# Cross attention in seven-product form: the values with channels on the partitions, turned by VectorE and ScalarE

## The chip, the cores and the metric

The kernel runs on one core of a Trainium2 chip. A core has a matrix engine (TensorE, PE in the profile, with its weight loads shown as PEld), a vector engine (VectorE, DVE), an activation engine (ScalarE, ACT), a general engine (GpSimd, POOL) and a queue engine (SyncE, SP), each with its own instruction stream; DMA queues move data between them. Engines wait for each other through semaphores. The metric is the device time of one execution in microseconds, of which the median over several runs is taken.

## The reference

There are 32 batch items, each with C = 256 channels and N = 1024 positions, all in float32. Cut to what matters:

```python
x_q = einsum('oc,bcn->bno', w_qk, y)          # y is ctx_2048
x_k = einsum('oc,bcn->bon', w_qk, x)
x_v = einsum('oc,bcn->bon', w_v, x) + b_v[None, :, None]
energy = einsum('bnc,bcm->bnm', x_q, x_k)
attention = softmax(energy, axis=-1)
attention = attention / (1e-07 + attention.sum(axis=1, keepdims=True))
x_r = einsum('bcn,bnm->bcm', x_v, attention)
x_r = relu(einsum('oc,bcn->bon', w_t, x - x_r) + b_t[None, :, None])
return x + x_r
```

## The kernel before

The weights are folded once at the start: `w_qk` with itself for the keys, and `w_t` with `w_v` for the values, so that the values already carry the last projection. Each batch item then has four products: keys (`Keys`, tiles `pg` and `gx`), values (`Values`, tiles `pu` and `ut`), energies (`Energy`, tiles `pe` and `e`, in four steps t = 0 to 3 of 128 rows per half) and the attention with the projected input (`Attention`, tiles `po`, `et`, `z`). Every one of them is cut into two by two blocks and computed with seven block products instead of eight. That is why every class has the steps p1 to p7 for products and c11, c12, c21, c22 for the blocks of the result: some products are accumulated onto others in the same PSUM bank, and between two of them ScalarE copies the bank to SBUF (`p1s`, `p5s`, `w`). A product that is accumulated onto a bank therefore waits until ScalarE has copied that bank.

The factors of the seven products are sums of blocks. For the input they are `xs` and `ys`, made by DMAs: SP loads copies, and GpSimd's queue then issues three DMAs that add (`accumulate`; the steps `xsteps` and `ysteps`). For the keys they are `gt`, for the values `us`, four additions on GpSimd each. For the attention they are `et`, additions on VectorE (`mix`).

The attention multiplies the values as weights (128 positions on the partitions, 128 channels as columns) with rows of `e` as moving data. It therefore wants the values with positions on the partitions. The kernel before makes them so at once: `Values.product` takes a 128 by 128 slice of the input as weights and the folded weights (128 columns) as moving data, four times for one block product. The bias of the values, a row of 256 numbers, is spread over the partitions (`uc`) and added to the whole tile `ut` by one accumulating DMA from GpSimd's queue (`bias`).

The order of the work is written out by hand: the wrappers `pe`, `dve`, `act` and `pool` (`InOrder`) keep each engine's instructions in the order in which the main loop calls them. All of them are recorded on line 77, so the profile's groups are told apart by tiles. The main loop over the batch items `b` first runs the energies of item b in the four steps t; at t = 0 the rest of the attention of the item before is mixed in (`before.end()`, `before.c21()`), and so is the next load of `x`. The keys of item b+1 follow, and its values, and then the attention of item b (`begin` and `run`), inside which the last value product (`u.p4`) and value blocks of item b+1 are made. For the last item, b = 31, there is nothing to prefetch: `more` is false, `before.end()` is not called at t = 0, and its attention and the rest of item 30's follow at the end.

In one item VectorE makes the energies' blocks (which also yield row minima and maxima), the weighted column sum `acc`, the column scale `rc`, the scaling of `e` (`normal`), the sums `et` and the output blocks `z`, which SP stores.

Of the kernel before, what the change touches and what calls it, by code (L numbers as in the profile page):

```python
# [9 lines left out]
F32 = mybir.dt.float32  # L10
# [6 lines left out]
def kernel(  # L17
# [29 lines left out]
    nc = tc.nc  # L47
    B, C, N = x.shape
    P = 128
# [16 lines left out]
    class InOrder:  # L66


        def __init__(self, engine):
            self.engine = engine  # L70
            self.last = None
# [37 lines left out]
    def accumulate(into, from_):  # L109
        return pool.dma_start(into, from_, accum_op=ALU.add)  # L110
# [13 lines left out]
    bv = scratch[:, 4, :KC].rearrange("p (k o) -> p k o", o=1)  # L124
    bt = const.tile([P, KC, 1], F32, name="bt")
    nbt = const.tile([P, KC, 1], F32, name="nbt")
    uc = const.tile([P, 1, C], F32, name="uc")
    nc.sync.dma_start(wqk, w_qk.rearrange("(k p) c -> p k c", p=P))
    load("x", 0, KC)
    nc.sync.dma_start(wt, w_t.rearrange("(k p) c -> p k c", p=P))  # L130
# [7 lines left out]
    few = const.tile([P, P], F32, name="few")  # L138
    dve.memset(few, 0.0)
    dve.memset(zeros, 0.0)  # L140
    parts = const.tile([P, NB, NG + 1], F32, name="parts")
    dve.memset(parts[:, :, NG], EPS)
    idle = bank("idle")
# [41 lines left out]
    def value_weights(wtT):  # L185

        pw = [bank(f"pw_{i}") for i in range(KC)]
        for i in range(KC):
            for k in range(KC):
                pe.matmul(  # L190
                    pw[i][:, :C], wv[:, k, ts(i, P)], wtT[:, k, :], start=(k == 0), stop=(k == KC - 1)
                )
        return lefts("wvtT", pw, -1.0)[1]

    bvb = scratch[:, 6, : KC * P].rearrange("p (k c) -> p k c", k=KC)

    def spread_bias():
        for k in range(KC):
            act.activation(bvb[:, k, :], few, AF.Identity, bias=bv[:, k, :], scale=1.0)

    def value_bias(wtT):

        pb = bank("pb")
        for k in range(KC):
            pe.matmul(
                pb[:, :C], bvb[:, k, :], wtT[:, k, :], start=(k == 0), stop=(k == KC - 1)
            )
        act.mul(uc[:, 0, :], pb[:, :C], -1.0)
        act.mul(nbt[:, :, 0], bt[:, :, 0], -1.0)

    up = ctx.enter_context(tc.tile_pool(name="up", bufs=2))
# [4 lines left out]
    def temp(tag, name):  # L216
        return cp.tile([P, MB], F32, tag=tag, name=name)

    def matmul(into, lhs, rhs, onto=False):
        pe.matmul(into, lhs, rhs, start=not onto, stop=True, skip_group_check=onto)  # L220
# [114 lines left out]
    class Values(Seven):  # L335


        def __init__(self, b, xr):
            super().__init__("u", b)
            self.xr = xr  # L340
            self.ut = up.tile([P, NT, C], F32, tag="ut", name=f"ut_{b}")

        def product(self, into, j, onto=False):
            for t in range(HT):
                pe.matmul(
                    into[:, ts(t, P)],
                    self.xr[j - 1][:, ts(t, P)],
                    u_left[j - 1],
                    start=(t == 0 and not onto),
                    stop=(t == HT - 1),  # L350
                    skip_group_check=True,
                )

        def tiles(self, p):
            return p.rearrange("p (t c) -> p t c", t=HT)

        def block(self, i, h):
            return self.ut[:, h * HT : h * HT + HT, ts(i, P)]

        def combine(self, i, h, in0, in1, op):  # L360
            dve.tensor_tensor(self.block(i, h), self.tiles(in0), self.tiles(in1), op)

        def c21(self):
            act.copy(self.block(1, 0), self.tiles(self.one))

        def bias(self):
            accumulate(self.ut, uc.to_broadcast([P, NT, C]))

        def factors(self):

            us = up.tile([P, 4, HT, P], F32, tag="us", name=f"us_{self.b}")
            s1, s2, s3, s4 = (us[:, j] for j in range(4))
            a11, a12, a21, a22 = (self.block(i, h) for i in range(2) for h in range(2))
            steps = [
                lambda: pool.tensor_tensor(s1, a21, a22, ALU.add),
                lambda: pool.tensor_tensor(s2, s1, a11, ALU.subtract),
                lambda: pool.tensor_tensor(s3, a11, a21, ALU.subtract),
                lambda: pool.tensor_tensor(s4, a12, s2, ALU.subtract),
            ]
            return (a11, a12, s4, a22, s1, s2, s3), steps  # L380

    class Energy(Seven):

# [55 lines left out]
    class Attention(Seven):  # L439
# [76 lines left out]
        def run(self, u, before=None):  # L516


            self.normal(0, 0)
            self.normal(1, 0)  # L520
            for j in range(HT // 2):
                self.normal(0, 1, j)
                self.mix(self.t1, self.b11, self.b12, ALU.add, j)
            if u:
                u.c22()
            if before:
                before.put()
                before.c21()
            self.normal(1, 1)
            self.mix(self.t2, self.t1, self.b22, ALU.subtract)  # L530
            self.epart(self.one, 1)
            self.p1s = self.biased(self.one, "p1s", bt[:, 0, :])
            self.epart(self.three, 2)
            self.epart(self.two, 5)
            self.p5s = self.biased(self.two, "p5s", bt[:, 1, :])
            self.xpart(self.one, 6, True)
            if u:
                u.p4()
                u.c21()
                u.c11()  # L540
                u.c12()
            self.c11()
            self.put()
            self.xpart(self.two, 3, True)
            self.epart(self.two, 3, (0, 1))
            self.epart(self.one, 6)
            self.w = self.biased(self.one, "w", nbt[:, 0, :])
            self.mix(self.t3, self.b12, self.b22, ALU.subtract)
            self.mix(self.t4, self.b21, self.t2, ALU.subtract)
            self.epart(self.two, 3, (2,))  # L550
            if u:
                self.epart(self.two, 3, (3,))
                self.c12()

        def end(self):
            self.xpart(self.one, 4, True)
# [57 lines left out]
    g.c11()  # L614
    g.p6()
    wtT, t_left = turned_weights()
    spread_bias()
    g.p3()
    g.c12()
    g.p7()  # L620
    g.c22()
    u_left = value_weights(wtT)
    g.p4()
    g.c21()
    rhs, _ = summed("y", 0)
# [6 lines left out]
    u = Values(0, xr)  # L632
    u.p1()
    u.p5()
    value_bias(wtT)
    u.p2()
    u.c11()
    u.p6()
# [6 lines left out]
    for b in range(B):  # L645
# [3 lines left out]
        for t in range(HT):  # L649
            now = Energy(b, t, lhs, rhs)  # L650
            pair.append(now)
            now.p1()
            if t > 0:
                pair[t - 1].exp(1)
            now.p5()
            if t == 0:
                if b == 0:
                    u.p4()
                    u.c21()
                    u.bias()  # L660
                    xsteps[1]()
                    xsteps[2]()
                elif more:
                    before.end()
                    before.c21()
                    load("x", b + 1)
                e = ep.tile([P, NT, N], F32, tag="e", name=f"e_{b}")
                acc = one.tile([P, N], F32, tag="acc", name=f"acc_{b}")
                ur, usteps = u.factors()
                first = 1 if more else 0  # L670
                for step in usteps[:first] + gsteps + usteps[first:]:
                    step()
            if t > 1:
                pair[t - 2].share(0)
            if t == 0:
                now.p6()
            now.p2()
            now.c11()
            if t == 1:
                pair[0].scale(1)  # L680
            if t > 1:
                pair[t - 1].share(1)
            if t > 0:
                now.p6()
            if t == 1:
                act.activation(acc, e[:, HT, :], AF.Copy, scale=scales[HT])
            if t > 0:
                pair[t - 1].p4()
                pair[t - 1].c21()
                pair[t - 1].exp(0)  # L690
            now.p3()
            now.c12()
            now.p7()
            now.c22()
            if more and b > 0:
                if t == 0:
                    xn, xsteps = summed("x", b + 1)
                else:
                    xsteps[t - 1]()
        last = pair[-1]  # L700

        if more:
# [46 lines left out]
        if more:  # L749
            now = Attention(b, xr, ur)  # L750
            now.begin()
            ysteps[0]()
            now.run(un)
            if b + 2 < B:
                now.xpart(now.one, 7, True)
                now.epart(now.one, 7)
                now.c22()
                now.put()
            now.put()
            ysteps[1]()  # L760
            un.bias()
            ysteps[2]()
            before = now
            xr, u = xn, un
        else:
            before.end()
            now.run(None, before)
            now.finish()
# [30 lines left out]
```

## Time and profile before

| | before |
|---|---|
| median of 3 runs | 2141.78 us (2140.91 to 2142.71) |
| the profiled execution: its time | 2142.63 us |
| the profiled execution: its span | 2140.9 us |
| PE busy | 2134.6 us (100%) |
| VectorE busy | 1769.1 us (83%) |
| ScalarE busy | 788.5 us (37%) |
| GpSimd busy | 612.7 us (29%) |
| granted TensorE clock | 1.000 |
| DMA moved | 282.58 MB |

The span runs from the first to the last instruction; 1.7 us of the profiled execution's time lie around it. "Idle before" in a row is the time for which the engine had nothing to do just before the instructions of the group, followed by what ended it. Times in a timeline are us from the span's start. A float32 product of 512 columns shows as two MATMUL rows, and a VectorE or ScalarE row can overlap the next one by some 0.1 us, since instructions are pipelined.

### The profile page before, as it was taken

The page shows a single profiled execution, that of the slowest core. Times are in us where ns is not written, and L with a number is a line of the kernel's source. Part 1 is how long each engine was busy: PE and PEld are TensorE (multiplying, and loading weights), DVE is VectorE, ACT ScalarE, POOL GpSimd, SP SyncE. Part 2 cuts the span into 40 slices and gives each one's busy share as a digit, 9 for nine tenths or more (in the row PEclk, how much of TensorE's full clock was granted, in tenths as well). Part 3 has the DMA queues.
Part 4 walks back from the last instruction along what each step waited for, and adds up shares of the span by engine and source line. Part 5 has one row for each costly group of instructions (what it writes and reads, how often), then busy time and mean ns, then how long its engine had stood idle before and what let it go on. Part 6 is the DMA issues. An engine that isn't in the chain of part 4 may idle for free.

```text
span 2140.9 us, 19900 instructions
## 1 busy us (share of the span) xinstructions
PE 2134.6 (100%) x6312; PEld 1058.5 (49%) x6312; DVE 1769.1 (83%) x3119; ACT 788.5 (37%) x1323; POOL 612.7 (29%) x488
## 2 busy tenths in 40 slices
PE   9999999999999999999999999999999999999999
PEld 5455444554445545455544555445554445544453
DVE  5889788898788887879878788778897888978898
ACT  5234443244432344333443234442244422444332
POOL 5322323313233133232232322323223233222320
PEclk9999999999999999999999999999999999999999
DMA  6555665556665556665566655665546655566540
GB/s 176 120 127 119 154 151 123 129 120 150 148 126 135 117 144 148 128 151 106 137 151 138 139 113 128 157 144 126 125 121 153 157 121 125 121 154 148 123 98 30
DMA packets 139048, 282.58 MB, mean 132 GB/s; under 512 B 9152, under 2 KB 42688, under 8 KB 138944
## 3 DMA queue, kind: packets, MB, share of 16 engines
q0 software_dynamic: 75936, 114.83, 34.0%
q1 hardware_dynamic: 63008, 166.48, 23.5%
q8 instruction: 50, 0.82, 0.2%
q14 instruction: 54, 0.44, 0.1%
HBM read 181.67 MB, written 33.55 MB: 101 GB/s over the span
## 4 chain that ended last, share of the span: by engine, by line
PE 98%; DVE 2%; issue 0%; DVEq 0%
PE po L77 44%; PE pe L77 35%; PE pu L77 9%; PE pg L77 9%; DVE e L77 1%; DVE acc L77 0%; PE idle L77 0%; DVE et L77 0%; PE pw L77 0%; DVE z L77 0%; DVE rc L77 0%; DVE sc L77 0%; PE pb L77 0%; DVE ri L77 0%; DVE parts L77 0%
## 5 line engine op out<-in xcount | busy, mean ns | idle before, releaser
L77 PE MATMUL pe<-gt,ys 128*128 128x512 f32 x768 | 392.1, 592 | 0.0
L77 DVE SCALAR_TENSOR_TENSOR e<-e,ri,rc 128x512 f32<-128x512 f32 x512 | 347.3, 745 | 1.1
L77 PE MATMUL po<-et,us 128*128 128x512 f32 x768 | 345.7, 593 | 0.5 <-DVE et L77 0.5
L77 DVE SCALAR_TENSOR_TENSOR acc<-e,ri,acc 128x1024 f32<-128x1024 f32 x224 | 288.6, 1288 | 8.0
L77 PE MATMUL pe<-gx,y 128*128 128x512 f32 x512 | 261.4, 592 | 0.0
L77 PEld LDWEIGHTS po<-et,us 128*128 128x128 f32 x768 | 145.5, 190 | 185.0 <-issue 166.8
L77 PEld LDWEIGHTS pe<-gt,ys 128*128 128x128 f32 x768 | 145.8, 190 | 183.4 <-issue 170.0
L77 PE MATMUL po<-e,ut 128*128 128x512 f32 x512 | 224.9, 592 | 0.0
L77 POOL TENSOR_TENSOR gt<-gx 128x512 f32<-128x512 f32 x64 | 81.6, 1274 | 391.4 <-DVE gx L77 391.4
L77 ACT COPY ep1s<-pe 128x512 f32<-128x512 f32 x128 | 75.0, 586 | 303.4 <-PE pe L77 298.9
L77 ACT ACTIVATE e<-e,nm 128x1024 f32<-128x1024 f32 x128 | 147.1, 1149 | 98.2 <-DVE nm L77 96.7
L77 DVE TENSOR_TENSOR et<-e 128x1024 f32<-128x1024 f32 x128 | 156.8, 1246 | 2.3
L77 PEld LDWEIGHTS po<-e,ut 128*128 128x128 f32 x512 | 97.3, 190 | 122.5 <-issue 106.2
L77 PEld LDWEIGHTS pe<-gx,y 128*128 128x128 f32 x512 | 97.2, 190 | 122.0 <-issue 114.1
L77 POOL TENSOR_TENSOR us<-ut 128x512 f32<-128x512 f32 x64 | 87.0, 1360 | 223.9 <-DMA ut<-uc 223.9
L77 ACT ACTIVATE e<-e,bias 128x1024 f32<-128x1024 f32 x128 | 147.4, 1152 | 1.6 <-DVE bias L77 1.5
L77 POOL DMA_DIRECT2D ut<-uc x32 | 50.5, 1579 | 338.0 <-DVE ut L77 281.1
L77 DVE TENSOR_TENSOR z<-z,x 128x512 f32<-128x512 f32 x31 | 46.3, 1492 | 118.3 <-ACT z L77 118.3
L77 DVE CUSTOM_DVE_ANT_0 e<-pe,ep1s 128x512 f32<-128x512 f32 x128 | 88.1, 688 | 64.2 <-ACT e L77 57.8
L77 PE MATMUL pe<-gx,ys 128*128 128x512 f32 x256 | 130.9, 593 | 0.5 <-DVE nm L77 0.5
L77 PE MATMUL pe<-gt,y 128*128 128x512 f32 x256 | 130.8, 592 | 0.0
L77 PE MATMUL po<-e,us 128*128 128x512 f32 x256 | 120.5, 592 | 0.0
(115 smaller groups left out, 3265.5 us busy)
## 6 DMA issues: line engine op xcount, KB each, us to landing
y<-in_ctx_dram SPq DMA_DIRECT2D x32, 1024.0 KB, 5.0
ut<-uc POOLq DMA_DIRECT2D x32, 1024.0 KB, 9.6
out_dram<-z SPq DMA_DIRECT2D x128, 256.0 KB, 2.3
x<-in_x_dram SPq DMA_DIRECT2D x31, 1024.0 KB, 6.2
xs<-in_x_dram SPq DMA_DIRECT2D x62, 512.0 KB, 4.6
ys<-in_ctx_dram SPq DMA_DIRECT2D x62, 512.0 KB, 4.2
xs<-in_x_dram POOLq DMA_DIRECT2D x31, 512.0 KB, 8.1
xs<-xs POOLq DMA_DIRECT2D x31, 512.0 KB, 5.0
```

Of the source, the lines that this page charges most:

```text
L77: self.last = getattr(self.engine, name)(*args, **kwargs)
```

## The change

The values are made with channels on the partitions, as the keys are: `Values.product` uses the folded weights as stationary data and 512 columns of the input as moving data, one product instead of four. The bias is then one number per partition, so ScalarE adds it while it copies the banks (`bu`, `nbu`, made at the start by `value_bias`), and `uc`, its spreading and the accumulating DMA are gone.

The attention still wants positions on the partitions. `turn` therefore has VectorE transpose the four value blocks in squares of 32 by 32 into the tile `turned`: four instructions of 128x512, behind the output block c12 in `Attention.run`. `move` then puts each group of 32 partitions where it belongs: 16 copies of 32x16x32 back into `ut`. For b = 0 SP issues them as 16 DMAs. For every other item ScalarE makes them in the energies of that item at t = 0: 6 ahead of p1's copy, 4 behind p5's copy, 6 behind c22.

GpSimd's order changes with it: a copy of one column (`behind`) makes its additions `gt` wait for VectorE's `t4`; then come the first accumulating DMA for `xs` and the four additions `us`, at the end of t = 0 in place of its beginning. The other two accumulating DMAs for `xs` are issued at t = 2 and t = 3 (before, the three were issued at t = 1, 2 and 3).

```diff
--- before.py
+++ after.py
@@ -124,7 +124,8 @@
     bv = scratch[:, 4, :KC].rearrange("p (k o) -> p k o", o=1)
     bt = const.tile([P, KC, 1], F32, name="bt")
     nbt = const.tile([P, KC, 1], F32, name="nbt")
-    uc = const.tile([P, 1, C], F32, name="uc")
+    bu = const.tile([P, KC, 1], F32, name="bu")
+    nbu = const.tile([P, KC, 1], F32, name="nbu")
     nc.sync.dma_start(wqk, w_qk.rearrange("(k p) c -> p k c", p=P))
     load("x", 0, KC)
     nc.sync.dma_start(wt, w_t.rearrange("(k p) c -> p k c", p=P))
@@ -138,6 +139,7 @@
     few = const.tile([P, P], F32, name="few")
     dve.memset(few, 0.0)
     dve.memset(zeros, 0.0)
+    behind = const.tile([P, 1], F32, name="behind")
     parts = const.tile([P, NB, NG + 1], F32, name="parts")
     dve.memset(parts[:, :, NG], EPS)
     idle = bank("idle")
@@ -192,20 +194,20 @@
                 )
         return lefts("wvtT", pw, -1.0)[1]
 
-    bvb = scratch[:, 6, : KC * P].rearrange("p (k c) -> p k c", k=KC)
-
-    def spread_bias():
-        for k in range(KC):
-            act.activation(bvb[:, k, :], few, AF.Identity, bias=bv[:, k, :], scale=1.0)
-
     def value_bias(wtT):
 
         pb = bank("pb")
-        for k in range(KC):
-            pe.matmul(
-                pb[:, :C], bvb[:, k, :], wtT[:, k, :], start=(k == 0), stop=(k == KC - 1)
-            )
-        act.mul(uc[:, 0, :], pb[:, :C], -1.0)
+        for i in range(KC):
+            for k in range(KC):
+                pe.matmul(
+                    pb[:, i : i + 1],
+                    wtT[:, k, ts(i, P)],
+                    bv[:, k, :],
+                    start=(k == 0),
+                    stop=(k == KC - 1),
+                )
+        act.mul(nbu[:, :, 0], pb[:, :KC], 1.0)
+        act.mul(bu[:, :, 0], pb[:, :KC], -1.0)
         act.mul(nbt[:, :, 0], bt[:, :, 0], -1.0)
 
     up = ctx.enter_context(tc.tile_pool(name="up", bufs=2))
@@ -335,40 +337,52 @@
     class Values(Seven):
 
 
+
         def __init__(self, b, xr):
             super().__init__("u", b)
             self.xr = xr
-            self.ut = up.tile([P, NT, C], F32, tag="ut", name=f"ut_{b}")
+            self.ut = up.tile([P, KC, MH, MB], F32, tag="ut", name=f"ut_{b}")
 
         def product(self, into, j, onto=False):
-            for t in range(HT):
-                pe.matmul(
-                    into[:, ts(t, P)],
-                    self.xr[j - 1][:, ts(t, P)],
-                    u_left[j - 1],
-                    start=(t == 0 and not onto),
-                    stop=(t == HT - 1),
-                    skip_group_check=True,
-                )
-
-        def tiles(self, p):
-            return p.rearrange("p (t c) -> p t c", t=HT)
+            matmul(into, u_left[j - 1], self.xr[j - 1], onto)
+
+        def bias(self, tag):
+            return {"p1s": bu[:, 0, :], "w": nbu[:, 0, :], "p5s": bu[:, 1, :]}[tag]
+
+        def kept(self, p, tag):
+            s = temp(tag, f"u{tag}_{self.b}")
+            act.activation(s, p, AF.Identity, bias=self.bias(tag), scale=1.0)
+            return s
 
         def block(self, i, h):
-            return self.ut[:, h * HT : h * HT + HT, ts(i, P)]
+            return self.ut[:, i, h]
 
         def combine(self, i, h, in0, in1, op):
-            dve.tensor_tensor(self.block(i, h), self.tiles(in0), self.tiles(in1), op)
+            dve.tensor_tensor(self.block(i, h), in0, in1, op)
 
         def c21(self):
-            act.copy(self.block(1, 0), self.tiles(self.one))
-
-        def bias(self):
-            accumulate(self.ut, uc.to_broadcast([P, NT, C]))
+            act.activation(self.block(1, 0), self.one, AF.Identity, bias=bu[:, 1, :], scale=1.0)
+
+        def turn(self):
+
+            self.turned = one.tile([P, KC * MH, MB], F32, tag="turned", name=f"turned_{self.b}")
+            for i in range(KC):
+                for h in range(MH):
+                    dve.transpose(self.turned[:, i * MH + h], self.block(i, h))
+            self.moves = [(a, g) for a in range(NG) for g in range(NG)]
+
+        def move(self, count, by):
+
+            from_ = self.turned.rearrange("p b (k c) -> p (b k) c", c=G32)
+            to = self.ut.rearrange("p i h (k c) -> p (i h k) c", c=G32)
+            from_, to = (v.rearrange("p (k g) c -> p k g c", g=NG) for v in (from_, to))
+            for a, g in self.moves[:count]:
+                by(to[ts(g, G32), :, a, :], from_[ts(a, G32), :, g, :])
+            self.moves = self.moves[count:]
 
         def factors(self):
 
-            us = up.tile([P, 4, HT, P], F32, tag="us", name=f"us_{self.b}")
+            us = up.tile([P, 4, MB], F32, tag="us", name=f"us_{self.b}")
             s1, s2, s3, s4 = (us[:, j] for j in range(4))
             a11, a12, a21, a22 = (self.block(i, h) for i in range(2) for h in range(2))
             steps = [
@@ -377,7 +391,10 @@
                 lambda: pool.tensor_tensor(s3, a11, a21, ALU.subtract),
                 lambda: pool.tensor_tensor(s4, a12, s2, ALU.subtract),
             ]
-            return (a11, a12, s4, a22, s1, s2, s3), steps
+            return [
+                f.rearrange("p (t c) -> p t c", t=HT)
+                for f in (a11, a12, s4, a22, s1, s2, s3)
+            ], steps
 
     class Energy(Seven):
 
@@ -551,6 +568,7 @@
             if u:
                 self.epart(self.two, 3, (3,))
                 self.c12()
+                u.turn()
 
         def end(self):
             self.xpart(self.one, 4, True)
@@ -614,12 +632,12 @@
     g.c11()
     g.p6()
     wtT, t_left = turned_weights()
-    spread_bias()
     g.p3()
     g.c12()
     g.p7()
     g.c22()
     u_left = value_weights(wtT)
+    value_bias(wtT)
     g.p4()
     g.c21()
     rhs, _ = summed("y", 0)
@@ -632,7 +650,6 @@
     u = Values(0, xr)
     u.p1()
     u.p5()
-    value_bias(wtT)
     u.p2()
     u.c11()
     u.p6()
@@ -649,6 +666,8 @@
         for t in range(HT):
             now = Energy(b, t, lhs, rhs)
             pair.append(now)
+            if t == 0 and b > 0:
+                u.move(6, act.copy)
             now.p1()
             if t > 0:
                 pair[t - 1].exp(1)
@@ -657,18 +676,22 @@
                 if b == 0:
                     u.p4()
                     u.c21()
-                    u.bias()
+                    u.turn()
+                    u.move(16, nc.sync.dma_start)
                     xsteps[1]()
                     xsteps[2]()
-                elif more:
+                else:
+                    u.move(4, act.copy)
+                if b > 0 and more:
                     before.end()
                     before.c21()
                     load("x", b + 1)
                 e = ep.tile([P, NT, N], F32, tag="e", name=f"e_{b}")
                 acc = one.tile([P, N], F32, tag="acc", name=f"acc_{b}")
-                ur, usteps = u.factors()
-                first = 1 if more else 0
-                for step in usteps[:first] + gsteps + usteps[first:]:
+                if before is not None:
+
+                    pool.tensor_copy(behind, before.t4[:, HT - 1, :1])
+                for step in gsteps:
                     step()
             if t > 1:
                 pair[t - 2].share(0)
@@ -692,11 +715,16 @@
             now.c12()
             now.p7()
             now.c22()
-            if more and b > 0:
-                if t == 0:
+            if t == 0:
+                u.move(6, act.copy)
+                ur, usteps = u.factors()
+                if more and b > 0:
                     xn, xsteps = summed("x", b + 1)
-                else:
-                    xsteps[t - 1]()
+                    xsteps[0]()
+                for step in usteps:
+                    step()
+            elif more and b > 0 and t > 1:
+                xsteps[t - 1]()
         last = pair[-1]
 
         if more:
@@ -758,7 +786,6 @@
                 now.put()
             now.put()
             ysteps[1]()
-            un.bias()
             ysteps[2]()
             before = now
             xr, u = xn, un
```

## The prediction

> **What bounds the kernel now.** I read the page's engine totals first, then the chain that ended last, then one item on the timeline, engine by engine, and last the two odd items at the ends. The totals and the chain's shares say that TensorE is never idle:
>
> ```profile
> PE 2134.6 (100%) x6312; PEld 1058.5 (49%) x6312; DVE 1769.1 (83%) x3119; ACT 788.5 (37%) x1323; POOL 612.7 (29%) x488
> ...
> PE 98%; DVE 2%; issue 0%; DVEq 0%
> ```
>
> The chain in order of time gives the price of one product. Four key products (8 records) take 3.43, 0.858 each; five value products (40 records) take 4.46, 0.892 each:
>
> ```profile
> 1110.96 3.43 PE pg L77 x8
> 1114.40 4.46 PE pu L77 x40
> ```
>
> So an item takes 70 x 0.858 + 7 x 0.892 = 66.3 us, and 1060.38 to 1126.72 (ScalarE's `op1s` of two items) is 66.34: no stall is left. Anything removed from PE is gained only if no other engine is late instead.
>
> VectorE comes next. From 1111.00, where it waits for p4 of t = 3, it runs without a gap until the second half of `et`; the weights that need it are loaded late, yet the next product is on time:
>
> ```profile
> 1111.00 0.75 DVE L77 CUSTOM_DVE_ANT_0 e<-pe,zeros,nm 128x512 f32<-128x512 f32 x1
> ...
> 1130.05 1.22 DVE L77 TENSOR_TENSOR et<-e 128x1024 f32<-128x1024 f32 x1
> ```
>
> ```profile
> 1131.33 0.19 PEld L77 LDWEIGHTS po<-et,us 128*128 128x128 f32 x1 [0.38 <-DVE et L77]
> ```
>
> A load normally shows 0.24 of idle, so this one is 0.14 late. In the first item the same load is 0.42 late (0.66 against 0.24), and its six products take 2.84 instead of 2.74: 0.10 lost, so 0.32 of lateness is free, and 0.18 of that is unused in an ordinary item.
>
> **The values' products.** Seven per item, 0.034 saved on each: 0.24 per item, 7.7 over 32. Six of the seven lie between 1111.00 and 1131.33, so PE comes 0.21 earlier to a VectorE that does not. 0.18 is free; 0.03 becomes a stall. Left per ordinary item: 0.21. Items 1 to 30 give 6.3. Item 0 uses up its free lateness already and gives only the seventh product, but the seven ahead of the loop give 0.24: together 0.3. In the prologue `pb` (17.59 to 18.46, 0.87) becomes four products of one column; between nothing and 0.87 saved, I take 0.4, since a record does not vanish with its columns. Gain 7.0.
>
> **The bias.** Four ScalarE copies per item turn from 0.586 to 0.687 (`op1s`' row, which has a bias too). `up1s` ends 0.1 later at 1116.07; p6 on that bank starts at 1116.91. The others have the same 0.8. Nothing. The accumulating DMA and GpSimd's wait for it go, and nothing on the path waited for them.
>
> **The transposes** go behind c12 on VectorE, where it idles:
>
> ```profile
> 1077.44 0.68 DVE L77 TENSOR_TENSOR z<-po,ow 128x512 f32<-128x512 f32 x1
> 1080.96 0.69 DVE L77 TENSOR_TENSOR z<-op5s,po 128x512 f32<-128x512 f32 x1 [2.84 <-PE po L77]
> ```
>
> The nearest row transposes 1024 columns, and at full price while GpSimd adds:
>
> ```profile
> 1119.44 1.25 DVE L77 STREAM_TRANSPOSE rc<-sc 128x1024 f32<-128x1024 f32 x1
> ```
>
> ```profile
> 1119.04 1.26 POOL L77 TENSOR_TENSOR gt<-gt,gx 128x512 f32<-128x512 f32 x1
> ```
>
> Half of it is 0.60 to 0.72, start to start 0.64: 1078.04 + 4 x 0.64 + 0.08 = 1080.7, inside the hole. Queued behind them are c22 and the two `put`s, with idle time until 1087.69 after them. Cost on VectorE's path: 0; without that hole it would be 2.6 per item.
>
> The Trainium skill speaks against this choice: "VectorE: DVE Perf Modes", sections "The three transpose paths" and "Rules for kernel authors", sends a full 128x128 transpose to TensorE, because VectorE turns only 32x32 blocks. The trace has it: the prologue's four transposes `pt` took 0.44 of PE (11.07 to 11.51), 0.11 each. By the rule 16 per item would put 1.8 on the engine that is never idle, 56 us in all; by the rows the way chosen costs the path nothing.
>
> **The moves.** ScalarE around the items' border:
>
> ```profile
> 1081.86 0.59 ACT L77 COPY ep1s<-pe 128x512 f32<-128x512 f32 x1 [6.16 <-PE pe L77]
> 1082.73 0.58 ACT L77 COPY ep5s<-pe 128x512 f32<-128x512 f32 x1 [0.28 <-PE pe L77]
> 1086.97 0.69 ACT L77 ACTIVATE z<-po,bt 128x512 f32<-128x512 f32 x1 [3.65 <-PE po L77]
> 1087.83 0.59 ACT L77 COPY ew<-pe 128x512 f32<-128x512 f32 x1 [0.17 <-PE pe L77]
> 1091.32 0.58 ACT L77 COPY ep1s<-pe 128x512 f32<-128x512 f32 x1 [2.90 <-PE pe L77]
> 1091.80 1.15 ACT L77 ACTIVATE e<-e,bias 128x1024 f32<-128x1024 f32 x1
> ```
>
> No row has a ScalarE copy from SBUF across partitions. The nearest is a copy of 512 from PSUM: 0.586, the next starting 0.48 later (1091.32, 1091.80). Reading SBUF adds 0.02 (`xb` 0.711 against 0.687). So 0.48 to 0.61 apart; I take 0.50, as all rows here overlap. All moves need all four transposes: start 1080.75. Six moves, the copies of p1 and p5, four moves: 1080.75 + 10 x 0.50 + 2 x 0.48 = 1086.7, and `z` is due at 1086.8 (PE 0.2 earlier). p1's copy is late, but p6, which waits for it, comes only at 1086.77, behind item b-1's last five products. After `ew` (1087.65) six moves: 1087.65 + 0.48 + 3.0 = 1091.13, p1's copy of t = 1 due at 1091.1. p6 of t = 1 starts at 1092.6, so that copy may start as late as 1091.87. With moves m apart it starts at 1082.77 + 16m: a stall from m = 0.57. At 0.50: 0.
>
> **GpSimd.** The new copy `behind` waits for VectorE's `t4` (1077.52); `gt`, the first `xs` DMA and `us` are queued behind it. `gt` still moves from 1083.35 to 1077.7, earlier than its users (p3 and p7 at 1088.5 and 1089.3), and off the `put`s that it lengthens now (2.36 for two, against 1.37). The first `xs` DMA needs SP's loads (landing at 1089.5, SP's issues being no later than now), then `us` runs from 1091.2 to 1096.3; VectorE's next operation with two SBUF inputs, `acc`, is at 1097.56, so they miss each other by 1.2. 0.
>
> **Item 0.** Two transposes wait for the block of 24.89; VectorE's next, 26.73, slips by 0.1 ahead of a wait of 1.65. SP issues 16 DMAs (0.35 each by its rows, 6 us) from 27; `us` was at 38.5, its first use is at 68.4. 0.
>
> **Item 31** has no cover. There `before.end()` is not called, so p6 of t = 0 comes straight after p5, at 2073.24, half way through the four records of the PE row, while VectorE is still at `et`:
>
> ```profile
> 2067.95 5.47 DVE L77 TENSOR_TENSOR et<-e 128x1024 f32<-128x1024 f32 x2
> 2073.34 2.35 DVE L77 TENSOR_TENSOR et<-e,et 128x1024 f32<-128x1024 f32 x2
> ```
>
> ```profile
> 2072.38 2.03 PE L77 MATMUL pe<-gt,ys 128*128 128x512 f32 x4
> ```
>
> Without GpSimd's collision (5.47 for 2.35; `behind` removes it) `et` ends at 2072.5, the transposes at 2075.7, six moves at 2078.8, p1's copy at 2079.35, p6 at 2079.5: 6.3 of stall, behind which everything is queued. Four moves ahead of `ew` add 0.4 at p7. Stalls of 0.25 there today are swallowed. Loss 6.4.
>
> **Sum.** 2142.63 - 7.0 + 6.4 = 2142.0 for the profiled execution, whose time is 0.85 above the median of the runs: 2141.2. A measurement of this kernel can tell about 0.2%, 4.3 us, from no change.
>
> **Rivals.** *ScalarE overruns (slower).* Place: the last six moves of t = 0 ahead of p1's copy of t = 1, from m = 0.57. At 0.586 the copy is 0.28 late, 8.4 us over 30 items, 2149.6; at 0.61 0.66 late, 20 us, 2161. For it: no row has this form. Against: consecutive ScalarE rows all overlap by 0.1. The same 1.1 us of spare time (16 x 0.07) is eaten if the transposes are 0.9 apart. Chance 0.20.
> *The last item does not stall (faster).* If ScalarE reached p1's copy in time the sum would be 2134.8. For it: the same moves are hidden in 30 items. Against: VectorE's `et` alone reaches 2072.5. Chance 0.08.
> *Item 0's DMAs are late.* They go in runs of 128 bytes; each us past about 63, where `us` must begin, is lost once: up to 10 us, 2151. For: no row shows such a DMA above 72 bytes and below 1 KB. Against: 30 us of cover. Chance 0.10, half of it inside 4.3 us.
>
> **Numbers.** The forecast has 0.62. Its own range, from 0.1 per item either way, is 2138 to 2145: 0.50 unchanged, 0.05 faster, 0.07 slower. With the rivals: faster 0.05 + 0.08 = 0.13, same 0.50 + 0.05 = 0.55, slower 0.07 + 0.20 + 0.05 = 0.32. The range of 8 in 10 runs from 2136, which leaves out the second rival, to 2151, which takes in the third and the near end of the first.
>
> **What would show it.** Right: `pu` products at 0.858, transposes near 0.7 behind c12, moves 0.50 apart, items of 66.1, and a ScalarE row `ep1s` with PE waiting some 6 us near 2070. Wrong: items above 66.4 with PE waiting for ScalarE at t = 1, VectorE rows of `acc` longer than 1.29, GpSimd's first `us` after 63, or no wait in item 31.

## The result, and the profile after

The changed kernel takes 2180.6 us (median of 6 runs, 2179.43 to 2181.54), beside 2141.98 us of the kernel before (6 runs measured together with them). The ratio is 1.018 with a 95% interval of 1.0167 to 1.0193: slower by 38.6 us, where 2141.2 us, no change, was predicted. The profiled execution has a span of 2177.7 us at a granted clock of 0.998.

The totals and the shares of the chain, from the page of the changed kernel:

```profile
PE 2145.1 (99%) x4972; PEld 933.7 (43%) x4972; DVE 1793.1 (82%) x3247; ACT 1096.0 (50%) x1818; POOL 540.0 (25%) x487
PE 69%; ACT 17%; DVE 11%; issue 2%; ACTq 0%; DVEq 0%
```

TensorE still looks busy for 99% of the span, and its busy time has even grown with 1340 instructions fewer, since rows behind a wait are drawn longer (1.13 for 1.02 in the row of p6 below). What tells is the chain. Before, 98% of it was TensorE. Now ScalarE has 17% and VectorE 11%, and among the lines on the page `ACT ut` alone has 14%: the moves decide when the kernel ends. Their group, and the products that wait for ScalarE (columns: busy time and mean ns of one, then the idle time before them and what ended most of it):

```profile
L77 PE MATMUL pe<-gt,ys 128*128 128x512 f32 x768 | 398.7, 601 | 26.4 <-ACT ep1s L77 18.8
L77 ACT COPY ut<-turned 32x512 f32<-32x512 f32 x496 | 305.3, 615 | 164.5 <-DVE turned L77 158.3
```

One move lasts 0.615 on the average, and 496 of them take 305.3. That is 0.615 each also when busy time is divided by their number, so they do not overlap at all. ScalarE around the border of two items, from its timeline; these rows answer to the six shown in "The moves":

```profile
1093.84 3.76 ACT L77 COPY ut<-turned 32x512 f32<-32x512 f32 x6 [5.12 <-DVE turned L77]
1097.62 0.59 ACT L77 COPY ep1s<-pe 128x512 f32<-128x512 f32 x1
1098.10 0.59 ACT L77 COPY ep5s<-pe 128x512 f32<-128x512 f32 x1
1098.72 2.50 ACT L77 COPY ut<-turned 32x512 f32<-32x512 f32 x4
1101.24 0.69 ACT L77 ACTIVATE z<-po,bt 128x512 f32<-128x512 f32 x1
1101.82 0.58 ACT L77 COPY ew<-pe 128x512 f32<-128x512 f32 x1
1102.42 3.74 ACT L77 COPY ut<-turned 32x512 f32<-32x512 f32 x6
1106.19 0.58 ACT L77 COPY ep1s<-pe 128x512 f32<-128x512 f32 x1
```

No row has idle time before it from the first move on: for 12.4 us ScalarE never catches up. The two copies `ep1s` and `ep5s` still start 0.48 apart, as before. The moves start 0.628 apart: 0.617 long, and the next one 0.011 after its end. TensorE pays for it at p6 of t = 1:

```profile
1106.83 1.13 PE L77 MATMUL pe<-gt,ys 128*128 128x512 f32 x2 [0.61 <-ACT ep1s L77]
```

An item now takes 67.297 (66.336 before). From the starts of its matmuls, p7 of t = 0 comes 0.27 late (`ew` at 1101.82 waits its turn behind four moves and `z`) and p6 of t = 1 0.88 late: 1.15 lost per item, of which the cheaper products give some back. VectorE's transposes stand where they were meant to, in the hole ahead of `z`:

```profile
1091.27 2.48 DVE L77 STREAM_TRANSPOSE turned<-ut 128x512 f32<-128x512 f32 x4
1093.98 0.69 DVE L77 TENSOR_TENSOR z<-op5s,po 128x512 f32<-128x512 f32 x1 [0.23 <-PE po L77]
```

Four of them take 2.48, start to start 0.593, and 0.23 of the hole of 2.84 is left. Item 31 shows the wait that was predicted for it, here on TensorE (p6 of t = 0) and on ScalarE:

```profile
2108.22 2.04 PE L77 MATMUL pe<-gt,ys 128*128 128x512 f32 x2 [6.94 <-issue]
```

```profile
2103.75 3.76 ACT L77 COPY ut<-turned 32x512 f32<-32x512 f32 x6 [4.85 <-DVE turned L77]
```

The hold costs more than its length. The product behind it is slow too:

```profile
2110.05 1.52 PE L77 MATMUL pe<-gx,y 128*128 128x512 f32 x2
```

The granted TensorE clock was 0.53 from 2104 to 2108, 0.50 from 2108 to 2111 and back at 1.00 from 2112 on. The four records from 2108.22 on start 0.98, 0.85 and 0.86 apart, and the next one 0.50 later, where 0.43 is usual: 1.4 us are lost there.

### The profile page after: what moved, and what is told of

Read it like the earlier page. It is cut to its first block, busy times and chain, and to the rows that moved or that the text cites. A ratio compares the mean times of both kernels' runs of the same rounds, so it can differ in the third digit from the quotient of the medians.

```text
span 2177.7 us, 17656 instructions
## 1 busy us (share of the span) xinstructions
PE 2145.1 (99%) x4972; PEld 933.7 (43%) x4972; DVE 1793.1 (82%) x3247; ACT 1096.0 (50%) x1818; POOL 540.0 (25%) x487
## 4 chain that ended last, share of the span: by engine, by line
PE 69%; ACT 17%; DVE 11%; issue 2%; ACTq 0%; DVEq 0%
PE po L77 27%; PE pe L77 24%; ACT ut L77 14%; PE pg L77 9%; PE pu L77 9%; DVE et L77 4%; DVE turned L77 3%; DVE e L77 1%; DVE z L77 1%; ACT z L77 1%; ACT ep1s L77 1%; ACT ep5s L77 1%; ACT ew L77 1%; DVE acc L77 0%; PE idle L77 0%
## 5 line engine op out<-in xcount | busy, mean ns | idle before, releaser
L77 PE MATMUL pe<-gt,ys 128*128 128x512 f32 x768 | 398.7, 601 | 26.4 <-ACT ep1s L77 18.8
L77 ACT COPY ut<-turned 32x512 f32<-32x512 f32 x496 | 305.3, 615 | 164.5 <-DVE turned L77 158.3
L77 PEld LDWEIGHTS pe<-gt,ys 128*128 128x128 f32 x768 | 141.0, 190 | 230.9 <-issue 178.6
L77 DVE TENSOR_TENSOR z<-z,x 128x512 f32<-128x512 f32 x31 | 21.5, 692 | 182.8 <-ACT z L77 182.8
L77 POOL DMA_DIRECT2D xs<-in_x_dram x62 | 65.8, 1061 | 363.2 <-PE pe L77 225.9
L77 ACT ACTIVATE op5s<-po,bt 128x512 f32<-128x512 f32 x32 | 22.0, 687 | 200.5 <-PE po L77 200.5
L77 ACT ACTIVATE op1s<-po,bt 128x512 f32<-128x512 f32 x32 | 22.0, 687 | 197.7 <-PE po L77 197.7
```

Of the source, the lines that this page charges most:

```text
L77: self.last = getattr(self.engine, name)(*args, **kwargs)
```

## The experiments

The theory from these rows: the price of a move was wrong (0.50 taken, 0.628 measured), and nothing else of size in an ordinary item. Its rivals: the transposes, the order on GpSimd or the last item cost more than was thought.

**What a copy of 32 partitions costs by itself.** A small kernel runs groups of eight copies back to back, with nothing else beside them. In most groups source and target keep their partitions from one copy to the next; `ff` and `fg` go to another group of 32 each time, as the moves do. Cut to the groups that the text names:

```python
"fa": A.copy(flat(t, j), bank)                                    # from PSUM, 128x512
"fb": A.copy(flat(t, j), flat(src, j))                            # from SBUF, 128x512
"fd": A.copy(flat(t, j)[32:64], flat(src, j)[:32])                # 0-31 to 32-63, always
"fe": A.copy(cut(t)[:32, :, j % 4, :], cut(src)[:32, :, j % 4, :])    # runs of 32, same partitions
"ff": A.copy(cut(t)[ts((j + 1) % 4, 32), :, 0, :], cut(src)[:32, :, j % 4, :])
"fg": ...                                                         # ff as an ACTIVATE
```

> This kernel computes nothing of the reference: it runs groups of eight equal instructions by themselves, on ScalarE fa (128x512 from PSUM), fb (128x512 from SBUF), fc (32x512, same partitions), fd (32x512, shifted by 32 partitions), fe (32x16x32 strided, same partitions), ff (strided and shifted, the move), fg (the move as an ACTIVATE), fh (128x512 from SBUF as an ACTIVATE), fi (128x16x32 strided), fj (PSUM and SBUF in turn), fk (ACTIVATE from SBUF with a bias column); on VectorE va (transposes), vb (the move as a copy), vc and vr (the move as other operations); on GpSimd ga. In the changed kernel a move takes 0.617 and the next starts 0.628 later, where the prediction had 0.50. Theory A, the shift of partitions ends the overlap: fb, fc, fe, fi 0.50 apart, fd, ff 0.63. Theory B, any copy from SBUF loses it: fb, fc, fd, fe, ff, fi all 0.63, fa 0.48. Theory C, the strided pattern: fe, ff, fi 0.63, fb, fc, fd 0.50. Theory D, the COPY instruction against ACTIVATE: fg and fh 0.5 apart whatever fb and ff do.

The groups of ScalarE in that run (busy time, mean ns of one):

```profile
L92 ACT COPY ff<-src 32x512 f32<-32x512 f32 x8 | 4.9, 616 | 0.1
L88 ACT COPY fd<-src 32x512 f32<-32x512 f32 x8 | 4.3, 613 | 0.0
L90 ACT COPY fe<-src 32x512 f32<-32x512 f32 x8 | 4.2, 611 | 0.0
```

Each of these copies lasts as long as the others, 0.61 to 0.62. The sum differs: eight copies of `ff` take eight times their length, 4.9, and those of `fd` and `fe` take 4.3 and 4.2, because each starts before the last one has ended. `fd` and `fe` start 0.52 apart, `ff` 0.63 to 0.64, and the ACTIVATE of the same form (`fg`) 0.64 to 0.65. A copy from PSUM starts 0.48 after the last, and one from SBUF over all 128 partitions 0.52. So neither 32 partitions, nor a shift between source and target, nor runs of 32 columns cost anything; none of the theories fits as it was put. What `ff` has and the others lack is that two neighbours differ in their partitions.

**Which change of partitions it is.** A second small kernel runs the sixteen moves in the kernel's order (`ka`), sorted by target (`kb`), sorted by shift (`kc`), and groups in which only the source (`ke`), only the target (`kf`) or both alike without any shift (`kg`) go from one copy to the next; `kh` and `ki` alternate a copy of 32 partitions with a copy from PSUM. `wa` and `wb` are `ka` and `kc` on VectorE.

> Again single groups that compute nothing of the reference. In the first such run only the two groups whose target partitions changed from one instruction to the next (ff, fg) followed each other 0.64 apart; a constant shift (fd) and a strided pattern (fe) gave 0.52. Now ScalarE copies of 32x16x32, unless said otherwise: ka in the kernel's order (16, the source group in the outer loop), kb sorted by target group, kc sorted by the shift (target less source group), kd the same shift with source and target both going on, ke fixed target and changing source (32x512), kf fixed source and changing target (32x512), kg no shift and a new group each time, kh copies of 128x512 from PSUM in turn with unshifted copies, ki the same in turn with shifted ones; wa and wb the kernel's order and the shift's order as VectorE copies. Theory A, a change of the shift ends the overlap: kc 0.52 but for six places, kd and kg 0.52, ke and kf 0.63, kh 0.5, ki 0.63. Theory B, a change of the target group does: kb 0.52 but for three places, ke 0.52, kd, kf and kg 0.63. Theory C, any change of the partitions: ka, kb, kc, kd, ke, kf, kg all 0.63. VectorE: 0.34 apart as in the first run (vb, a constant shift), or up to 0.41 if it loses its overlap too.

```profile
L86 ACT COPY ka<-src 32x512 f32<-32x512 f32 x16 | 9.8, 615 | 1.4 <-DVE src L54 1.0
L86 ACT COPY kc<-src 32x512 f32<-32x512 f32 x16 | 9.8, 615 | 0.2
L86 ACT COPY kg<-src 32x512 f32<-32x512 f32 x8 | 4.9, 613 | 0.1
```

All ScalarE groups, `kh` and `ki` included, lie 0.61 to 0.65 apart: 9.8 for 16 is 0.61 of busy time each, without overlap. The order does not matter (`kc` as `ka`), the shift does not matter (`kg` has none), and a change of the source alone or of the target alone is enough (`ke` and `kf`, 0.63 to 0.64). The theory that any change of the partitions between neighbours ends the overlap holds. The sixteen moves are sixteen different pairs, so no order of them gets it back.

**The products alone, and with the transposes.** Two versions leave the values where the products put them, so that their layout is not the one the attention needs: one without transposes and moves, one with the transposes.

```diff
# both: without the moves               # the first: also without
-    u.move(6, act.copy)                -    u.turn()
-    u.move(16, nc.sync.dma_start)
-    u.move(4, act.copy)
-    u.move(6, act.copy)
```

> The changed kernel without its transposes and moves; the attention then uses values that are not turned. What is left of the change is the products of 512 columns, the bias on ScalarE, and GpSimd's new order. Theory 1 (the moves on ScalarE are the whole loss): items of 66.13 (0.21 less than before), PE never waits for ScalarE, about 2135. Theory 2 (the transposes behind c12 make ScalarE and VectorE late): 2135 too. Theory 3 (the values' products or the new order of GpSimd bring nothing or lose): 2142 or more.

> The changed kernel with its transposes, without its moves (the values are turned into a tile that nobody reads). Theory 1: the transposes lie in VectorE's hole of 2.84, so the same 2135 as without them, within 1. Theory 2: most of the 38 us stay, above 2165.

Measured: 2136.92 us without both (ratio 0.9975, 0.9965 to 0.9984) and 2136.65 us with the transposes (0.9974, 0.9965 to 0.9984), beside 2142.10 of the kernel before. Items take 66.133 in both, 0.203 less than before, and there is no such hold in item 31. The transposes are free, and the products with all that belongs to them (bias, GpSimd's order) are worth some 5.3 us. The rest, 2180.6 - 2136.7 = 43.9 us, is the moves.

**Short moves.** The same instructions in the same order with the same waits, but each move copies a quarter of its columns (all but those of item 0), so that most of the values is left unmoved:

```diff
-    by(to[ts(g, G32), :, a, :], from_[ts(a, G32), :, g, :])
+    short = slice(0, 16 if self.b == 0 else 4)
+    by(to[ts(g, G32), short, a, :], from_[ts(a, G32), short, g, :])
```

> The changed kernel with the same instructions in the same order and with the same waits, but for every item after the first each of ScalarE's sixteen moves takes 4 runs of 32 columns instead of 16 (three quarters of the values are not moved). A move should take 0.3 instead of 0.617. It takes away ScalarE's time alone, where the run with ten moves also let GpSimd start its additions earlier. Theory 1 (the length of the moves on ScalarE): PE never waits for ScalarE at t = 0 and 1, items of 66.13, item 31 still waits 2.5 for the transposes and 1.9 for six short moves: 2136.9 + 4.5 = 2141.5. Theory 2 (the waits of the moves for VectorE, or the order, whatever their length): about 2178.

Measured: 2141.71 us, ratio 0.9999 (0.999 to 1.0008). The moves and item 31 in it:

```profile
L77 ACT COPY ut<-turned 32x128 f32<-32x128 f32 x496 | 146.6, 296 | 108.2 <-DVE turned L77 102.0
```

```profile
2070.97 1.77 PE L77 MATMUL pe<-gt,ys 128*128 128x512 f32 x2 [3.19 <-issue]
```

At 0.296 a move the stalls of the items are gone (items of 66.13), and of item 31 a wait of 3.2 is left in place of 6.9; with the slow products behind it, item 31 loses 4.8 (60.57 between the `op1s` of items 30 and 31, 55.75 without moves). Nothing but the length of a move was changed, so this is the term that decides. That the time is close to the one predicted is partly chance: the moves are shorter here than the 0.50 of the prediction, and item 31 loses less.

**Ten moves.** The last six moves are left out in all items but the first (part of the values stays unmoved), which should leave only the small stall at p7:

```diff
-                u.move(6, act.copy)
+                if b == 0:
+                    u.move(6, act.copy)
```

> The changed kernel without the last six of the sixteen moves of each item (a part of the values is left unturned). Theory 1: the wait of p6 at t = 1 (0.78 per item) goes, the wait of p7 at t = 0 (0.26 with its aftermath) stays, as does item 31's wait of 7: 2135 + 30 x 0.26 + 7 = 2150. Theory 2: the loss hangs on the transposes and not on the number of moves: about 2180.

This missed the expectation: 2177.59 us, ratio 1.0164 (1.0149 to 1.0179). ScalarE has idle time now, 2.14 us ahead of p1's copy of t = 1. The wait moved elsewhere, as the timelines of VectorE, GpSimd and TensorE show:

```profile
1102.31 2.71 DVE L77 TENSOR_TENSOR z<-z,x 128x512 f32<-128x512 f32 x1 [6.09 <-ACT z L77]
```

```profile
1102.71 1.74 POOL L77 TENSOR_TENSOR us<-ut 128x512 f32<-128x512 f32 x1
1104.53 1.61 POOL L77 TENSOR_TENSOR us<-us,ut 128x512 f32<-128x512 f32 x1
```

```profile
1109.12 1.12 PE L77 MATMUL pe<-gt,y 128*128 128x512 f32 x2 [0.81 <-ACT ep5s L77]
```

GpSimd's additions `us` wait for the moves. With six moves fewer they start at 1102.71, right on VectorE's addition `z`, which takes 2.71 in place of 0.69 (2.0 to 2.9 in 28 of the 31 items) and holds up c11, `bias`, ScalarE's `e` (1.88 of idle time ahead of it), its copy `ep5s` and so p3. In the changed kernel the same additions start 3.5 us later, at 1106.26. That reading was tested by putting the additions back where they were:

```diff
# on top of the ten moves
             now.p1()
+            if t == 1:
+                if b > 0:
+                    pool.tensor_copy(behind, now.p1s[:, :1])
+                for step in usteps:
+                    step()
...
-                for step in usteps:
-                    step()
```

> As the kernel of ten moves (the last six moves behind c22 are left out for all items but the first, so part of the values is wrong), but GpSimd's four additions us are held back until ScalarE's copy of p1 of t = 1, where they began in the changed kernel. Theory (ten moves missed because GpSimd's additions came 3.5 us earlier and ran against VectorE's addition to z): with that collision gone, p6 of t = 1 waits for nothing, p7 of t = 0 still waits some 0.2 to 0.26 for the copies that the first ten moves delay, and item 31 still waits some 7: 2136.9 + 30 x 0.24 + 7.1 = 2151.2, items of 66.37. Rival (the 2177.6 of ten moves was due to something else that the ten moves do, a wait between VectorE and ScalarE that stays): items stay at 66.4 to 67.9 and the time stays above 2170.

Measured: 2154.39 us, ratio 1.0056 (1.0039 to 1.0073), with items of 66.40. So the collision cost the ten moves some 23 us, and the six moves ahead of p1's copy of t = 1 cost the changed kernel 26 us, 2180.6 - 2154.4, as do 30 times the 0.88 at p6 of t = 1. TensorE's p6, p4 of t = 0 and p3 behind the place of the collision:

```profile
1094.32 1.02 PE L77 MATMUL pe<-gt,ys 128*128 128x512 f32 x2
1095.17 1.02 PE L77 MATMUL pe<-gx,ys 128*128 128x512 f32 x2
1096.03 1.02 PE L77 MATMUL pe<-gt,y 128*128 128x512 f32 x2
```

The starts are 0.86 apart without a wait, and VectorE's `z` takes 0.69 again. The time is 3 us above what was expected, less than its interval can tell; the items, 0.03 longer than expected, are 1 us of that, and item 31 is 1.5: it takes 64.34 from `op1s` to `op1s`, 8.6 more than without moves, where 7.1 was taken. Behind its hold, too, the granted clock was 0.50 (2083 to 2086.2).

**The last item by DMA.** In item 31 SP issues the moves, as in item 0, and ScalarE is left free:

```diff
-                u.move(6, act.copy)
+                if more:
+                    u.move(6, act.copy)
+                else:
+                    u.move(16, nc.sync.dma_start)
```

with the other two calls of item 31 left out.

> The changed kernel, but in item 31 SP issues the sixteen moves as DMAs, as in item 0; items 1 to 30 are unchanged. Theory (item 31 is a hold of its own, 6.94 at p6 of t = 0, some 0.5 at p7 and 0.30 at p6 of t = 1, and the other 30 items lose 1.14 to 1.18 each whatever item 31 does): 2180.6 - 7.1 to 7.7 = 2173.0 to 2173.5, and the long wait at the start of item 31's energies gone. Rival (item 31 is late anyhow, since VectorE's et and the transposes behind it set that time, or the DMAs land too late for us): at least half of it stays, 2177 or more.

Measured: 2171.86 us, ratio 1.0137 (1.0121 to 1.0152). That is 8.7 below the changed kernel, more than the 7.1 to 7.7 expected, and the items stay at 67.30. The traces give item 31's share: from the `op1s` of item 30 to that of item 31 it takes 55.60 here and 64.63 in the changed kernel, 9.0 more. Of that, 7.0 are lost at p6 of t = 0, 1.4 in the products at half the clock, and 0.6 at p6 of t = 1. (The spans of the two profiled executions differ by 7.7 only, since this run was already 1.2 later at the `op1s` of item 1.) TensorE in item 31 runs through; p5 and p6 of t = 0 are one row now:

```profile
2101.66 2.03 PE L77 MATMUL pe<-gt,ys 128*128 128x512 f32 x4
```

Item 31's hold is a cost of its own, some 9 us, and here the granted clock is 1.00 from 2095 to 2120.

**A version that beats both.** If moves on ScalarE cannot be short, most of them can go elsewhere: twelve of the sixteen as copies by VectorE in its wait of 6.09 for `z` (as in the row of the ten moves), four on ScalarE behind `ew`, and item 31's by DMA. Everything is computed.

```diff
-            self.moves = [(a, g) for a in range(NG) for g in range(NG)]
+            self.moves = sorted(((a, g) for a in range(NG) for g in range(NG)), key=lambda m: m[1] - m[0])
...
-            if t == 0 and b > 0:
-                u.move(6, act.copy)
...
-                else:
-                    u.move(4, act.copy)
+                elif not more:
+                    u.move(16, nc.sync.dma_start)
                 if b > 0 and more:
+                    u.move(12, dve.tensor_copy)
                     before.end()
                     before.c21()
...
-                u.move(6, act.copy)
+                u.move(4, act.copy)
```

> A version that keeps the whole computation: sorted by their shift, twelve of an item's moves are copies on VectorE, in its wait for z (4.8 between the last put and z's addition; 12 x 0.34 = 4.1), four stay on ScalarE behind ew, none stand ahead of p1's copy; item 31's moves are DMAs like item 0's. Theory 1: items of 66.13 and no wait in item 31, so about 2137, plus up to 3 where GpSimd's late additions of item 31 collide with VectorE. Theory 2 (the turned values cost their loss wherever the moves are made): above 2150.

Measured: 2135.82 us (2134.77 to 2137.3), ratio 0.9971 (0.996 to 0.9981), 6.4 us below the kernel before. Its VectorE and ScalarE at the border of two items:

```profile
1078.02 5.16 DVE L77 COPY ut<-turned 32x512 f32<-32x512 f32 x12
```

```profile
1083.58 2.50 ACT L77 COPY ut<-turned 32x512 f32<-32x512 f32 x4
1086.40 0.59 ACT L77 COPY ep1s<-pe 128x512 f32<-128x512 f32 x1 [0.33 <-PE pe L77]
```

VectorE's `z` follows at 1083.22: the twelve copies fill its wait, and ScalarE's copy of t = 1 waits for TensorE again, with 0.33 to spare. Items take 66.133, as with no moves at all.

## Why the prediction was wrong

**The step that failed is the price of a move, the "0.50 apart".** It was taken from rows in which all neighbours read and write the same partitions, and the argument for it was that "all rows here overlap". The moves are the only ScalarE instructions of the main loop whose partitions change from one to the next, and they are 0.628 apart. The upper bound of the prediction, 0.61, was the better reading for want of a row, though still too low by 0.018: an instruction's own length, without credit for an overlap that no row of its form shows. The Trainium skill has the pattern for the other engine: "VectorE: DVE Perf Modes", section "Two Vector instructions with no wait between them", says that an instruction whose input or output begins in another group of 32 partitions than the last one's is held until all earlier ones have finished. VectorE's copies agree (0.42 long and 0.43 to 0.45 apart in the groups `wa` and `wb` and 0.43 in the last version, 0.335 at constant partitions), and ScalarE behaves alike in these runs, of which that page does not speak.

**The formula around it held.** At 0.628 it has p1's copy of t = 1 start at 1082.77 + 16 x 0.628 = 1092.82, 0.95 behind the latest start that costs nothing. It left out one thing: a move behind `ep5s` and behind `ew` also starts after their end, 0.616 and 0.601 after their start in place of 0.48. That adds 0.25, so 1.20 late, beside 1.15 measured as 0.27 at p7 and 0.88 at p6. That the first part falls on p7 of t = 0 was not seen; the delay is the same, taken in two places.

**The rival that came true** is the one given 0.20, ScalarE's overrun, at its named place. Its worst case, 0.61, gave 2161. With the measured length its loss is not 20 us but 30 x 1.16 = 34.9 us (67.297 against 66.133).

**Item 31**: the hold was right in mechanism, and too small by the same price. Six moves of 0.628 in place of 0.50 turn the 6.3 of the prediction into 7.07; from the starts of the matmuls 7.0 was lost at p6. A second term was left out: the granted clock of 0.50 around the hold, which made the products behind it 1.4 longer. With 0.6 at p6 of t = 1, item 31 loses 9.0 us against the run in which DMAs make these moves; 6.4 was predicted.

**The products** gain 0.203 per item (0.21 predicted). In all 5.2 us are measured without the moves, 7.0 predicted; the intervals, some 2 us either way, cover the difference. One part of it is seen in the profile: `pb` was to save 0.4 and saved 0.06, since from its start to the next product's its eight records of one column take 0.81 where four of 256 took 0.87. The rest stays open.

**The transposes** are free, as predicted (0.593 apart for 0.64 predicted, both inside the hole). **GpSimd** costs nothing as predicted, but by less than it seemed: `us` ends at 1111.3, 0.4 ahead of `acc`, where 1.2 was expected. The ten moves show what lies on the other side, 23 us. **Item 0**: SP took 15.2 us to issue the sixteen DMAs and not 6, and `us` was made by 51.5, still ahead of 63; that rival fell.

The sum with measured terms: 2136.9 (no moves) + 34.9 (30 items) + 9.0 (item 31) = 2180.8, beside 2180.6 measured.

## What to carry to other kernels

An overlap between neighbours belongs to the pair, not to the instruction: for a form that no row shows, take the full length of one as the likely price, and ask first what changes between one instruction and the next. When a formula gives the spare time per instruction (here a stall from 0.57 apart, with bounds of 0.48 and 0.61), the decision lies in that one number, and it deserves more than the odds of a side case. Moving work away from an overrun engine also moves all that waits for it: look at what the freed waiters run into before counting the gain. And a hold of the bounding engine can cost more than its length: here 7.0 us of it came with 1.4 us of slow products.

## What the runs showed of the hardware

- ScalarE's copies of 512 columns from SBUF start 0.52 apart when neighbours use the same partitions, and 0.61 to 0.65 apart when source or target partitions change, whatever their order and whether or not they shift the data. On VectorE the same change costs some 0.10 (0.335 to 0.43 to 0.45, for copies of 32x512).
- TensorE's granted clock fell to about 0.50 at the holds of item 31 (one of 6.94 in the changed kernel, one of 3.19 with short moves) and was back at 1.00 some 3 to 4 us after the products had resumed; in between, records started 0.85 apart in place of 0.43. Without a hold (item 31 by DMA) it was 1.00 there.
- An addition of two SBUF tiles on VectorE took 2.71 in place of 0.69 when GpSimd's additions ran beside it (1.59 in the kernel before, beside other additions), and GpSimd's took 1.74 and 1.61 in place of 1.26. The Trainium skill, "SBUF — State Buffer", section "SBUF: two separate sides", describes one shared pair of ports that goes to whichever of the two starts first and blocks the other for that whole instruction. The rows agree that both engines lose, but not with this order as it stands: `z` starts at 1102.31, 0.40 ahead of the first addition, and yet ends at 1105.02, 0.57 after that addition. How the turns were taken is not shown.
- Sixteen SBUF-to-SBUF DMAs of 64 KB in runs of 128 bytes took SP 15.2 to issue in item 0 and some 11 in item 31 (in the run with the last item by DMA), where the prediction had read 0.35 each from rows with longer runs.
